# Sums of the second attention layer as two float32r products, and a reordered start, in a two-layer attention kernel

## The chip, the cores and the metric

One core of one Trainium2 chip runs the whole kernel. The metric is the device time of one execution in microseconds, from the first to the last instruction with what lies around them. All times below are in microseconds (us).

## The reference

Eight images of 32 x 32 positions (N = 1024 tokens) with 512 channels go through two layers. Each layer is x + attention(group norm(x)). The first has 16 heads of 32 channels, a bias-free qkv projection and an output projection w_proj. The second has 4 heads of 128 channels, projections Wq, Wk, Wv, Wo, and adds relative position logits (one term from the column offset, one from the row offset) to the scores ahead of the softmax:

```python
# layer 0
attn = softmax((q * SCALE) @ k.T);  x = x + (attn @ v) @ w_proj + b_proj
# layer 1
q = groupnorm(x) @ Wq * scale
scores = q @ k + relative_logits(q, pos_emb_w, pos_emb_h)
x = x + (softmax(scores) @ v) @ Wo
```

Everything is float32. The part that the change touches is the denominator of the second layer's softmax: for each query the sum of exp(score) over 1024 keys.

## The kernel before

**Layout.** Activations lie transposed in SBUF, channels on the 128 partitions, in four chunks (cc) of 1024 tokens. Every projection is a two-by-two block product done in seven instead of eight products (`seven`, with the combinations that `forms` makes on DVE, L332 to L335). Its matmuls are all issued in `by_columns` (L312), 32 columns of weights at a time. The weight combinations are made once at the start: `Matrix.fetch` loads a 512 x 512 weight (L135), `Matrix.add_up` subtracts quarters (four operations, L146) and stores the result to DRAM (L148) for later streaming (`Stream`, L198).

**Batches.** The eight images (batches) go through as a software pipeline. While attention_0 (first layer) of one batch runs, pieces of the neighbours' projections are dealt in between by costs (`side_by_side`). attention_1 (second layer) yields a cost of 0 in every step, so that it runs as one block, with attention_0 standing still. Woven into the block is only the loading of the next batch (`load`: DVE transposes L710, statistics L248/L249, group norm L274 to L292, forms), a piece every few steps. Blocks 1 to 6 in time have such a load beside them; the last two have not.

**attention_1.** Eight groups: head h (4) times half c of the queries (2), and in each eight steps j over the keys. A step is, on PE: two products into a PSUM bank, k times q (L647, fp32) and the position logits (L648, float32r); then, for the step before, v times e into the accumulator acc (L659, fp32). ACT takes exp of the bank into e (L650). DVE adds the e's of a group up in es (L668, L670). When a group's eight steps are through, ACT copies acc to q (L673), the product of an all-ones matrix and es (L679) sums es over the partitions, and `normalise` follows: ACT copies the sums (su, L495), DVE transposes, inverts, checks and transposes back (L497 to L513), POOL multiplies q by it (L517). The banks for ps, acc and sums come from a pool "bank" of three; the tag "ps", a tile of four banks, holds attention_0's logits. The snapshots su and tu have a tag "rec" with two buffers.

**Order.** The program is emitted in Python order, generators being stepped as described; then a scheduler sets each engine's own order, by what is ready. Each engine takes its list strictly in turn and waits at semaphores. In the resulting lists before the change, L679 stands on PE after the first L659 of the next group; at the end of a block (`run` of the last `finish`) it stands right after the last L659. After the block PE goes on with a projection (x_q, x_wp or x_wo) or, for the last batch, with x_wo, whose later products y_wo need the forms f_ao of the normalised q.

**Start.** `load_first` loads batch 0 by rows (x_rows), turns it on PE into PSUM banks (L737), copies the banks to x0T (ACT L745, DVE L747), takes statistics, puts x0T away to DRAM on SP's queue (`put_away`, L217, four stores d<-x0T) and runs group norm (L292 in place on x0T, four times) and forms. Then WV0's, WQ0's and WK0's combinations are made: WV0's on POOL, the others' on DVE, each stored by POOL's queue. The first products (x_v, y_v, z_v: the values of batch 0) follow; their a_v is L372.

**The end.** After the last block: x_wo products, then su, tu, rc, su (L495 to L513), POOL's L517 on q, the forms f_ao, and y_wo, z_wo. `Onto.gather` adds products to x2T on POOL (L431) and DVE (L436), and the rows go out (L835, L840).

Of the kernel before, what the change touches and what calls it, by code (L numbers as in the profile page):

```python
# [9 lines left out]
F32 = mybir.dt.float32  # L10
F32R = mybir.dt.float32r
# [6 lines left out]
P = 128  # L18
# [9 lines left out]
def quick_path(  # L28
# [23 lines left out]
    nc = tc.nc  # L52
# [3 lines left out]
    CC = C // P  # L56
    NT = N // P
    NB = 512
# [3 lines left out]
    HB = P // D0  # L62
# [4 lines left out]
    consts = ctx.enter_context(tc.tile_pool(name="consts", bufs=1))  # L67
    mem = ctx.enter_context(tc.tile_pool(name="mem", bufs=1))
    small = ctx.enter_context(tc.tile_pool(name="small", bufs=1))
    psum = ctx.enter_context(tc.tile_pool(name="psum", bufs=1, space=PSUM))  # L70
# [4 lines left out]
    def block(name, shape=None, dtype=F32):  # L75
        return mem.tile(shape or [P, CC, N], dtype, tag="block", name=name, bufs=BLOCKS)

    def chunks(block):
        return [block[:, i, :] for i in range(CC)]

    def bank(name, shape=None):
        return psum.tile(shape or [P, NB], F32, tag="bank", name=name, bufs=3)
# [1 line left out]

    ident = consts.tile([P, P], F32, tag="ident", name="ident")
    make_identity(nc, ident)
    ones = consts.tile([P, P], F32, tag="ones", name="ones")
    nc.gpsimd.memset(ones, 1.0)
    bproj_sb = consts.tile([P, CC], F32, tag="bproj_sb", name="bproj_sb")
    with nc.allow_non_contiguous_dma(reason="512 values, once"):  # L90
        nc.gpsimd.dma_start(bproj_sb, b_proj.rearrange("(cc p) -> p cc", p=P))
# [212 lines left out]
    in_place = [False]  # L304

    half_done = [None]

    def by_columns(out, weights, moving, start, stop, open_sum=False):

        for g in range(P // 32):  # L310
            columns = slice(32 * g, 32 * g + 32)
            ins = nc.tensor.matmul(  # L312
                out[columns, :],
                weights[:, columns],
                moving,
                start=start,
                stop=stop,
                skip_group_check=open_sum,
            )
            if in_place[0]:  # L320
                tc.keep_in_program_order(ins)
        in_place[0] = False

    def forms(x, name):


        a11, a12 = x[:, :HC, :NB], x[:, HC:, :NB]
        a21, a22 = x[:, :HC, NB:], x[:, HC:, NB:]
        s1, s2, s4 = [
            mem.tile([P, HC, NB], F32, tag=f"form{i}", name=f"f{i}_{name}", bufs=1) for i in (1, 2, 4)  # L330
        ]
        nc.vector.tensor_add(s1, a21, a22)  # L332
        nc.vector.tensor_sub(s2, s1, a11)  # L333
        nc.vector.tensor_sub(a21, a11, a21)
        nc.vector.tensor_sub(s4, a12, s2)  # L335
        return [a11, a12, s4, a22, s1, s2, a21]

    def snapshot(tag, name):
# [150 lines left out]
    def normalise(dst, acc_sums, name):  # L489

        su = mem.tile([P, NB], F32, tag="rec", name=f"su_{name}", bufs=2)
        nc.scalar.copy(su, acc_sums)  # L495
        turned = mem.tile([P, NB], F32, tag="rec", name=f"tu_{name}", bufs=2)
        nc.vector.transpose(turned, su)  # L497
        few = turned.rearrange("p (t c) -> p t c", c=32)[:, :, 0]
        rec = mem.tile([P, NB // 32], F32, tag="few", name=f"rc_{name}", bufs=2)
        nc.vector.reciprocal(rec, few)  # L500
        at = check_at[0]
        check_at[0] += 1
        nc.vector.tensor_tensor_reduce(
            out=few,
            in0=few,
            in1=rec,
            op0=ALU.add,
            op1=ALU.max,
            scale=1.0,
            scalar=0.0,  # L510
            accum_out=checks[:, at : at + 1],
        )
        nc.vector.transpose(  # L513
            su.rearrange("p (t c) -> p t c", c=32),
            rec.unsqueeze(2).to_broadcast([P, NB // 32, 32]),
        )
        nc.gpsimd.tensor_tensor(dst, dst, su, op=ALU.mult)  # L517
# [119 lines left out]
    def attention_1(q, k, v, posT, b):  # L637

        steps = [(h, c, j) for h in range(H1) for c in range(NH) for j in range(NT)]
        state = {}  # L640

        def front(h, c, j):
            name = f"1_{b}_{h}_{c}_{j}"
            ps = bank(f"ps_{name}")
            keys = slice(j * P, (j + 1) * P)
            queries = slice(c * NB, (c + 1) * NB)
            nc.tensor.matmul(ps, k[h][:, keys], q[:, h, queries], start=True, stop=False)  # L647
            nc.tensor.matmul(ps, sel_flat[:, keys], posT[:, h, queries], start=False, stop=True)  # L648
            e = mem.tile([P, NB], F32, tag="e1", name=f"e_{name}", bufs=3)
            nc.scalar.activation(e, ps, AF.Exp, scale=1.0 / math.sqrt(D1))  # L650
            return e

        def back(h, c, j, e):
            name = f"1_{b}_{h}_{c}_{j}"
            if j == 0:
                state["acc"] = bank(f"acc_{name}")
                state["first"] = e
            acc = state["acc"]
            nc.tensor.matmul(  # L659
                acc,  # L660
                v[:, j, h * D1 : (h + 1) * D1],
                e,
                start=(j == 0),
                stop=(j == NT - 1),
            )
            if j == 1:
                state["esum"] = mem.tile([P, NB], F32, tag="es1", name=f"es_{name}", bufs=2)
                nc.vector.tensor_add(state["esum"], state["first"], e)  # L668
            elif j > 1:
                nc.vector.tensor_add(state["esum"], state["esum"], e)  # L670
            if j < NT - 1:
                return
            nc.scalar.copy(q[:, h, c * NB : (c + 1) * NB], acc)  # L673
            state["ended"] = (h, c, state["esum"])

        def finish(h, c, esum):
            name = f"1_{b}_{h}_{c}"
            su = bank(f"sums_{name}")
            nc.tensor.matmul(su, ones, esum, start=True, stop=True)  # L679
            normalise(q[:, h, c * NB : (c + 1) * NB], su, name)  # L680

        pending = None
        for at in steps:
            e = front(*at)
            ended = state.pop("ended", None)
            if pending is not None:
                back(*pending)
            pending = (*at, e)
            if ended is not None:
                finish(*ended)  # L690
            yield 0
        back(*pending)
        yield 0
        finish(*state.pop("ended"))

    def load(b, st):

# [21 lines left out]
    def load_first(st):  # L719

        rows = block("x_rows", [P, NT, C])
        for t in range(NT):
            queue = nc.scalar if t % 2 else nc.sync
            queue.dma_start(rows[:, t, :], xf[0, t * P : (t + 1) * P, :])
        WV0.fetch(nc.sync)
        x = block("x0T_0")
        xT = chunks(x)
        for h in range(NH):
            if h == 0:
                whole = psum.tile([P, CC, NB], F32, tag="ps", name="turned_0", bufs=1)  # L730
                banks = [whole[:, cc, :] for cc in range(CC)]
            else:
                banks = [bank(f"turned_1_{cc}") for cc in range(CC - 1)]
                banks.append(psum.tile([P, NB], F32, tag="acc", name="turned_1", bufs=1))
            for t in range(NT // NH):
                for cc in range(CC):
                    nc.tensor.transpose(  # L737
                        banks[cc][:, t * P : (t + 1) * P],
                        rows[:, h * (NT // NH) + t, cc * P : (cc + 1) * P],
                        ident,  # L740
                    )
            for cc in range(CC):
                part = xT[cc][:, h * NB : (h + 1) * NB]
                if h == 0 or cc % 2:
                    nc.scalar.copy(part, banks[cc])  # L745
                else:
                    nc.vector.tensor_copy(part, banks[cc])  # L747

        idle = psum.tile([P, CC, NB], F32, tag="ps", name="idle", bufs=1)
        for t in range(6):  # L750
            nc.tensor.matmul(idle[:, t % CC, :], ident, rows[:, t, :], start=True, stop=True)
        for cc in (1, 0, 3, 2):
            statistics(st, xT, cc, "0_0")
        st["kept"] = put_away(xT, "0_0")
        run(group_norm(st, xT, "0_0"))
        st["xn"] = forms(x, "xn0_0")

    def before_first(st):
# [99 lines left out]
    def run(part):  # L858
        for _ in part:
            pass  # L860
# [53 lines left out]

    states = [{} for _ in range(B)]
    load_first(states[0])
    WV0.add_up(nc.gpsimd, nc.gpsimd, keep=True)
    for m in (WQ0, WK0):
        m.fetch(nc.sync)
        m.add_up(nc.vector, nc.gpsimd, keep=True)  # L920
    fill_sel()
    stream = Stream(plan)

# [12 lines left out]
    for b in range(B + 1):  # L936
        rest, total = [], 0
# [531 lines left out]
```

## Time and profile before

| what | value |
|---|---|
| runs | 3903.57, 3906.62, 3903.42 (median 3903.57) |
| profiled execution | 3902.0 |
| its span, first to last instruction | 3900.2 |
| busy: PE, DVE, ACT, POOL | 3806.4, 2517.3, 1725.1, 621.7 |
| granted TensorE clock, mean | 0.995 |
| L679 sums, records x mean | 128 x 0.592 |
| L648 float32r logits, records x mean | 512 x 0.794 |
| L650 exp on ACT, count x mean | 512 x 0.598 |
| L670 es on DVE, count x mean | 384 x 0.760 |
| L495 copy on ACT, count x mean | 128 x 0.586 |

An fp32 matmul leaves two records (two halves that follow each other), a float32r matmul one. Matmuls are pipelined, so the length of a record isn't what a matmul costs: that is read from the distance of two starts. In a timeline line the columns are start, duration, engine, source line, operation, output and inputs, partitions x elements, count, and in brackets the idle time before it and what ended it. In a line of waits the three numbers are the total, how many, and the longest. The lines of the kernel's profile carry the numbers of the code above (L679 is line 679).

### The profile page before, as it was taken

Reading aid. Unit: us, or ns where it says so; the run is one execution under the profiler, and the core shown is the slowest. Engines: PE = TensorE matmul, PEld = TensorE weight load, DVE = VectorE, ACT = ScalarE, POOL = GpSimd, SP = SyncE. Lnnn points to the kernel's source line nnn. Section 1 sums busy time; section 2 is a strip of 40 time slices with the busy share of each in tenths; the row PEclk is TensorE's granted clock in tenths of the full one; section 3 lists DMA queues with packets and bytes.
Section 4 is the critical chain, followed back from the end, with each engine's and each line's share of the span. In section 5 each row is a group of like instructions: output and inputs, shape, how many; then the busy total and the mean of one; then the engine's idle time right before and its main releaser. Section 6 shows DMA issues by size and latency. Waiting matters only on the chain. (4 is left out here: it accounts for less than half of the span.)

```text
span 3900.2 us, 79833 instructions
## 1 busy us (share of the span) xinstructions
PE 3806.4 (98%) x34478; PEld 1370.9 (35%) x34478; DVE 2517.3 (65%) x2905; ACT 1725.1 (44%) x1767; POOL 621.7 (16%) x400
## 2 busy tenths in 40 slices
PE   8999899999999999999999999999999999999998
PEld 3222244232442224432343323433234332244353
DVE  5777675576745867468664686656865568754544
ACT  2554553445434454344544445344453445643132
POOL 1341001121101211012111121111210112011101
PEclk9999999999999999999999999999999999999999
DMA  5221120133202322023120241103311123110401
GB/s 172 86 95 51 40 61 3 39 117 70 59 5 63 107 57 55 12 91 84 46 55 17 92 94 40 44 24 97 88 45 32 31 92 69 32 63 18 124 17 23
DMA packets 482984, 234.73 MB, mean 60 GB/s; under 512 B 269600, under 2 KB 461376, under 8 KB 481600
## 3 DMA queue, kind: packets, MB, share of 16 engines
q1 hardware_dynamic: 470992, 213.74, 20.3%
q0 software_dynamic: 2608, 13.70, 1.0%
q8 instruction: 274, 4.49, 0.5%
q10 hardware_dynamic: 9024, 2.10, 0.3%
q14 instruction: 86, 0.70, 0.1%
HBM read 170.72 MB, written 58.72 MB: 59 GB/s over the span
## 5 line engine op out<-in xcount | busy, mean ns | idle before, releaser
L540 ACT ACTIVATE e<-ps 128x2048 f32<-128x2048 f32 x512 | 961.7, 1878 | 844.6 <-PE ps L532 605.9
L562 DVE TENSOR_TENSOR es<-es,e 128x2048 f32<-128x2048 f32 x384 | 890.8, 2320 | 400.2 <-ACT e L540 397.4
L532 PE MATMUL ps<-q,k 32*64 32x512 f32 x8192 | 577.2, 615 | 36.4 <-ACT e L540 36.3
L650 ACT ACTIVATE e<-ps 128x512 f32<-128x512 f32 x512 | 305.9, 598 | 585.9 <-PE ps L648 549.1
L551 PE MATMUL acc<-e,v 128*32 128x512 f32 x4096 | 547.1, 606 | 0.4 <-ACT su L495 0.4
L647 PE MATMUL ps<-q,k 128*128 128x512 f32 x1024 | 523.6, 593 | 0.4 <-DVE posT L633 0.4
L659 PE MATMUL acc<-e,v 128*128 128x512 f32 x1024 | 521.9, 592 | 0.0
L517 POOL TENSOR_TENSOR q<-q,su 128x512 f32<-128x512 f32 x128 | 214.3, 1674 | 1564.8 <-DVE su L513 1538.1
L670 DVE TENSOR_TENSOR es<-es,e 128x512 f32<-128x512 f32 x384 | 291.8, 760 | 264.0 <-ACT e L650 262.5
L648 PE MATMUL ps<-posT,sel 128*128 128x512 f32 x512 | 406.6, 794 | 0.0
L647 PEld LDWEIGHTS ps<-q,k 128*128 128x128 f32 x1024 | 193.6, 190 | 246.2 <-issue 240.6
L532 PEld LDWEIGHTS ps<-q,k 32*64 32x64 f32 x8192 | 120.4, 130 | 432.4 <-ACT e L540 217.0
L659 PEld LDWEIGHTS acc<-e,v 128*128 128x128 f32 x1024 | 193.1, 189 | 146.7 <-issue 105.0
L551 PEld LDWEIGHTS acc<-e,v 128*32 128x32 f32 x4096 | 81.5, 108 | 413.4 <-issue 365.8
L560 DVE TENSOR_TENSOR es<-e,e 128x2048 f32<-128x2048 f32 x64 | 174.7, 2730 | 39.7 <-ACT e L540 39.7
L497 DVE STREAM_TRANSPOSE tu<-su 128x512 f32<-128x512 f32 x128 | 90.6, 708 | 136.2 <-ACT su L495 136.0
L495 ACT COPY su<-sums 128x512 f32<-128x512 f32 x128 | 75.1, 586 | 151.3 <-PE sums L572 83.4
L648 PEld LDWEIGHTS ps<-posT,sel 128*128 128x128 f32 x512 | 97.3, 190 | 122.5 <-issue 122.5
L668 DVE TENSOR_TENSOR es<-e,e 128x512 f32<-128x512 f32 x64 | 44.2, 691 | 145.7 <-ACT e L650 145.7
L633 DVE TENSOR_TENSOR posT<-pp,posT 32x512 fp32r<-32x512 f32 x128 | 112.0, 875 | 32.2 <-ACT posT L628 30.8
L421 POOL TENSOR_TENSOR k<-b_k,p_k 128x512 f32<-128x512 f32 x32 | 51.2, 1599 | 477.0 <-ACT p_k L386 474.9
L628 ACT CAST posT<-pp 32x512 fp32r<-32x512 f32 x128 | 106.0, 828 | 45.2 <-PE pp L615 44.1
(195 smaller groups left out, 4510.1 us busy)
## 6 DMA issues: line engine op xcount, KB each, us to landing
w_qkv<-ws_qkv SPq DMA_DIRECT2D x168, 128.0 KB, 2.5
d<-x0T SPq DMA_DIRECT2D x32, 512.0 KB, 3.6
x1T<-d SPq DMA_DIRECT2D x32, 512.0 KB, 5.5
d<-x1T SPq DMA_DIRECT2D x32, 512.0 KB, 3.6
x2T<-d SPq DMA_DIRECT2D x32, 512.0 KB, 5.9
w_qkv<-in_L_conv_w_qkv SPq DMA_DIRECT2D x126, 128.0 KB, 2.2
out<-ot SPq DMA_DIRECT2D x240, 64.0 KB, 2.0
xs<-in_x SPq DMA_DIRECT2D x224, 64.0 KB, 2.6
```

Of the source, the lines that this page charges most:

```text
L517: nc.gpsimd.tensor_tensor(dst, dst, su, op=ALU.mult)
L532: nc.tensor.matmul(ps[some, r, :], k[m][rows, j * P + 64 * i : j * P + 64 * i + 64], q[m][rows, h * NB : (h + 1) * NB], start=True, stop=True,
L540: nc.scalar.activation(e, ps, AF.Exp, scale=D0 ** -0.5)
L551: nc.tensor.matmul(acc[r * D0 : (r + 1) * D0, :], v[:, j, c0 : c0 + D0], e[:, r, :], start=(j == 0), stop=(j == NT - 1),)
L560: nc.vector.tensor_add(state["esum"], state["first"], e)
L562: nc.vector.tensor_add(state["esum"], state["esum"], e)
L633: nc.vector.tensor_sub(rest, logits, greater)
L647: nc.tensor.matmul(ps, k[h][:, keys], q[:, h, queries], start=True, stop=False)
L648: nc.tensor.matmul(ps, sel_flat[:, keys], posT[:, h, queries], start=False, stop=True)
L650: nc.scalar.activation(e, ps, AF.Exp, scale=1.0 / math.sqrt(D1))
L659: nc.tensor.matmul(acc, v[:, j, h * D1 : (h + 1) * D1], e, start=(j == 0), stop=(j == NT - 1),)
L670: nc.vector.tensor_add(state["esum"], state["esum"], e)
```

## The change

In `attention_1` the sum of es over the partitions is no longer one fp32 product. `finish` becomes a generator: one step after the group's end, ACT copies es into a float32r tile (sg, the rounded part) and DVE subtracts it (sr, the rest); two steps later, PE takes the sum as two float32r products, all-ones times sg and all-ones times sr, accumulated in one bank. That bank is the first of the tile with tag "ps". At the end of a block all of `finish` is run at once. In PE's list the pair stands after the fourth L659 of the next group; at the end of a block, after one matmul of the projection that follows. In ACT's list sg stands ahead of the next group's first exp, and su behind its fourth; in DVE's list sr stands behind the last es of its group, and tu to su some two to three steps later than before. sg and sr take buffers of the tag "rec". The all-ones tile gets the type float32r and is read as fp32 elsewhere.

At the start, all eight copies of the turned batch 0 to x0T are made on ACT (before: six on ACT, two on DVE), the statistics go over the chunks in the order 0, 2, 1, 3, and the weight combinations of WQ0 and WK0 on DVE are issued behind the last operation of the first forms (`issue_after`). In the lists this moves the eight L146 of DVE behind the forms, where four of them stood among statistics and group norm and two among the forms; it moves the load of WK0 on SP's queue ahead of the four stores d<-x0T, and POOL's second store of combinations behind rstd (L289). At the ends of the last two batches POOL's L431 on p_wo or p_wp stands ahead of the last L517 instead of behind it.

```diff
@@ -84,8 +84,9 @@
 
     ident = consts.tile([P, P], F32, tag="ident", name="ident")
     make_identity(nc, ident)
-    ones = consts.tile([P, P], F32, tag="ones", name="ones")
-    nc.gpsimd.memset(ones, 1.0)
+    ones_r = consts.tile([P, P], F32R, tag="ones", name="ones")
+    nc.gpsimd.memset(ones_r.bitcast(F32), 1.0)
+    ones = ones_r.bitcast(F32)
     bproj_sb = consts.tile([P, CC], F32, tag="bproj_sb", name="bproj_sb")
     with nc.allow_non_contiguous_dma(reason="512 values, once"):
         nc.gpsimd.dma_start(bproj_sb, b_proj.rearrange("(cc p) -> p cc", p=P))
@@ -304,6 +305,7 @@
     in_place = [False]
 
     half_done = [None]
+    last_form = [None]
 
     def by_columns(out, weights, moving, start, stop, open_sum=False):
 
@@ -332,7 +334,7 @@
         nc.vector.tensor_add(s1, a21, a22)
         nc.vector.tensor_sub(s2, s1, a11)
         nc.vector.tensor_sub(a21, a11, a21)
-        nc.vector.tensor_sub(s4, a12, s2)
+        last_form[0] = nc.vector.tensor_sub(s4, a12, s2)
         return [a11, a12, s4, a22, s1, s2, a21]
 
     def snapshot(tag, name):
@@ -675,23 +677,38 @@
 
         def finish(h, c, esum):
             name = f"1_{b}_{h}_{c}"
-            su = bank(f"sums_{name}")
-            nc.tensor.matmul(su, ones, esum, start=True, stop=True)
+
+            yield
+
+            greater = mem.tile([P, NB], F32R, tag="rec", name=f"sg_{name}", bufs=2)
+            nc.scalar.copy(greater, esum)
+            rest = mem.tile([P, NB], F32R, tag="rec", name=f"sr_{name}", bufs=2)
+            nc.vector.tensor_sub(rest, esum, greater.bitcast(F32))
+
+            yield
+            yield
+
+            su = psum.tile([P, HB, NB], F32, tag="ps", name=f"sums_{name}", bufs=1)[:, 0, :]
+            nc.tensor.matmul(su, ones_r, greater, start=True, stop=False)
+            nc.tensor.matmul(su, ones_r, rest, start=False, stop=True)
             normalise(q[:, h, c * NB : (c + 1) * NB], su, name)
 
         pending = None
+        ending = []
         for at in steps:
             e = front(*at)
-            ended = state.pop("ended", None)
             if pending is not None:
                 back(*pending)
             pending = (*at, e)
-            if ended is not None:
-                finish(*ended)
+            for part in ending:
+                next(part, None)
+            if "ended" in state:
+                ending = [finish(*state.pop("ended"))]
+                next(ending[0])
             yield 0
         back(*pending)
         yield 0
-        finish(*state.pop("ended"))
+        run(finish(*state.pop("ended")))
 
     def load(b, st):
 
@@ -739,17 +756,14 @@
                         rows[:, h * (NT // NH) + t, cc * P : (cc + 1) * P],
                         ident,
                     )
-            for cc in range(CC):
+            for cc in (0, 2, 1, 3):
                 part = xT[cc][:, h * NB : (h + 1) * NB]
-                if h == 0 or cc % 2:
-                    nc.scalar.copy(part, banks[cc])
-                else:
-                    nc.vector.tensor_copy(part, banks[cc])
+                nc.scalar.copy(part, banks[cc])
 
         idle = psum.tile([P, CC, NB], F32, tag="ps", name="idle", bufs=1)
         for t in range(6):
             nc.tensor.matmul(idle[:, t % CC, :], ident, rows[:, t, :], start=True, stop=True)
-        for cc in (1, 0, 3, 2):
+        for cc in (0, 2, 1, 3):
             statistics(st, xT, cc, "0_0")
         st["kept"] = put_away(xT, "0_0")
         run(group_norm(st, xT, "0_0"))
@@ -917,7 +931,9 @@
     WV0.add_up(nc.gpsimd, nc.gpsimd, keep=True)
     for m in (WQ0, WK0):
         m.fetch(nc.sync)
-        m.add_up(nc.vector, nc.gpsimd, keep=True)
+
+        with tc.issue_after(last_form[0].ins):
+            m.add_up(nc.vector, nc.gpsimd, keep=True)
     fill_sel()
     stream = Stream(plan)
 
```

## The prediction

> **What bounds the kernel now.** I read the busy shares first, then the chain of waits and PE's own list of waits, then the instruction groups and the timelines of the places that the change touches.
>
> ```profile
> PE 3806.4 (98%) x34478; PEld 1370.9 (35%) x34478; DVE 2517.3 (65%) x2905; ACT 1725.1 (44%) x1767; POOL 621.7 (16%) x400
> ```
>
> PE is busy for 98% of the span and the chain of waits runs along PE, so a saved PE slot is saved time, as long as nothing else comes late there. PE's waits are few:
>
> ```profile
> PE ps L532 <- ACT e L540: 36.3, 30, 7.6
> PE y_wo L312 <- DVE a_wo L372: 11.2, 9, 1.7
> PE x_v L312 <- issue: 9.3, 1, 9.3
> ...
> PE y_wo L312 <- DVE f_ao L333: 3.1, 1, 3.1
> ```
>
> The longest row belongs to attention_0, which the change leaves alone. The 9.3 us is the start, and the last row the end (3861 to 3865 us); both are touched. In attention_1 PE waits for nothing that counts. Its steps, from the PE timeline of the seventh group of batch 7:
>
> ```profile
> 3809.18 1.02 PE L659 MATMUL acc<-e,v 128*128 128x512 f32 x2
> 3810.04 1.02 PE L679 MATMUL sums<-es,ones 128*128 128x512 f32 x2
> 3810.90 1.02 PE L647 MATMUL ps<-q,k 128*128 128x512 f32 x2
> 3811.35 0.80 PE L648 MATMUL ps<-posT,sel 128*128 128x512 f32 x1
> 3811.99 0.59 PE L659 MATMUL acc<-e,v 128*128 128x512 f32 x1
> ```
>
> Ends overlap, so I price by starts. L679 starts 0.86 after L659, and L647 0.86 after L679: an fp32 product of 512 columns takes a slot of 0.857. From L647 (3810.90) to L659 (3811.99) is 1.09; less L647's own 0.857 leaves 0.233 for L648, the float32r product, though its record says 0.80. A group of eight steps repeats every 16.433 us = 8 x 1.947 + 0.857 (a step is 2 x 0.857 + 0.233).
>
> **What the skill says.** "FP8 and Floating Point Precision", TensorE Precision Notes: true FP32 takes four passes through the array, and reduced-precision FP32 reads a truncated value. The trace agrees: 0.857 / 0.233 = 3.7. "SBUF — State Buffer", Terms: VectorE and GpSimd share a port pair, held for a whole instruction, and "the loser fully blocks". The trace agrees: the L333 that starts at 595.34, while POOL's L517 runs from 595.00 for 1.56, takes 2.30 where its like takes 1.21. "PSUM — Partial Sum Buffer", Engine vs sequencer instructions: the queues of ScalarE, VectorE and GpSimd are strict FIFO. In the trace, too, the records of each keep the order of the instruction list; that rule decides steps 2 to 4 below.
>
> **Step 1, the 56 sums inside a block (8 batches, 7 each).** One fp32 product goes; two float32r products come, after the fourth L659 of the next group, two steps later. The idle bank they use is attention_0's logits tile, which is free in this block. 0.857 - 2 x 0.233 = 0.391, times 56 = **-21.9 us**. The trace has no two float32r products back to back. If the second overlaps less (0.32, midway to a full fp32 half), it is -17; if each is its 0.21 (a fourth of 0.857), -24.
>
> ScalarE gets a copy (sg, 0.59 as its other 512-column copies) and DVE a subtraction (sr, 0.60 to 0.69 as L670). Neither is a bound in the block: an exp of 0.60 each 1.947 us on ACT. What counts is the place in the queues (steps 2 to 4).
>
> **Step 2, the seven block ends before the last.** There the sums follow one product of the next projection, and the last es (L670) now has two operations behind it. Before:
>
> ```profile
> 682.65 0.69 DVE L670 TENSOR_TENSOR es<-es,e 128x512 f32<-128x512 f32 x1 [1.25 <-ACT e L650]
> 682.67 0.30 PEld L659 LDWEIGHTS acc<-e,v 128*128 128x128 f32 x2 [0.66 <-ACT e L650]
> 683.40 0.43 PEld L679 LDWEIGHTS sums<-es,ones 128*128 128x128 f32 x2 [0.43 <-DVE es L670]
> 683.64 1.02 PE L679 MATMUL sums<-es,ones 128*128 128x512 f32 x2
> ```
>
> The sums end their slot at 683.64 + 0.857 = 684.50. After: es ends 683.34; sg 683.42 to 684.01; sr 684.06 to 684.75; weights and handing over 0.29; the second float32r slot 0.23: 685.27. The cost is 0.77 each, and PE has only one matmul to put into it: 7 x 0.77 = **+5.4 us** (4 to 6).
>
> **Step 3, the last block's end.** Here su, tu, rc, su and POOL's L517 lead to the forms (L332, L333) for which y_wo waits. The sums come 0.77 later; the instruction order also puts POOL's L431 (x2T += p_wo) ahead of the last L517. L431 waits for the ACT copy p_wo (L367), which ended at 3859.93 and moves to about 3860.5; L431 1.27, then L517 1.28: 3863.1 instead of 3861.48. **+1.65 us** (0.8 to 3.3: PE's clock fell to half right after the 3.15 us gap there, and a longer gap may cost another such stretch). In batch 6 the same order of POOL is hidden behind other work of PE.
>
> **Step 4, sg stands in front of an exp.** In ACT's list sg stands ahead of the next group's first exp, and waits for es of step 7 on DVE. Queued behind it are that exp and the copy q (L673); PE's L659 waits for the exp. Elsewhere es of step 7 ends 0.72 after the last exp, in 58 of the 64 groups (the DVE and ACT timelines). sg then ends 0.72 + 0.08 + 0.59 = 1.39 after it; the next exp starts, in the trace, 1.35 after. A delay of 0.06 against 1.15 us that its L659 leaves: nothing. In the six blocks beside which the next batch is loaded (553 to 3052 us), the third group is different. DVE has the forms there:
>
> ```profile
> 597.56 0.68 DVE L670 TENSOR_TENSOR es<-es,e 128x512 f32<-128x512 f32 x1
> 598.16 1.21 DVE L334 TENSOR_TENSOR x0T<-x0T 128x1024 f32<-128x1024 f32 x1
> 599.30 0.68 DVE L670 TENSOR_TENSOR es<-es,e 128x512 f32<-128x512 f32 x1
> 599.90 1.21 DVE L335 TENSOR_TENSOR f_xn<-x0T,f_xn 128x1024 f32<-128x1024 f32 x1
> 601.04 1.48 DVE L670 TENSOR_TENSOR es<-es,e 128x512 f32<-128x512 f32 x2
> ```
>
> es ends 602.51, 2.05 after exp 7 (600.46); it hurt nobody, as the sums came two steps later. sg may start only then. With the lag L, sg ends L + 0.67 after exp 7, and PE is late by L + 0.67 + 0.02 - 1.35 - 1.08 (its 1.15 less 0.07 of handing over) = L - 1.74. What is L after the change? DVE gains sr of the group before (0.60), and the chain tu to su (1.8) with POOL's product behind it moves two steps later, so that the product meets L334 instead of L333 and costs its 1.1 where DVE has no idle time left (at L333 it had some 0.7 before). I take 2.05 + 0.60 + 0.35 = 3.0, a stall of 1.3, with a handing over of 0.1: 1.4 x 6 = **+8.4 us**. Ends: L unchanged 0.3 x 6 = 2; 0.60 + 1.1 more, 2.1 x 6 = 13.
>
> **Step 5, the start.** DVE loses two copies L747 (0.68 each) to ACT, which then has 8 instead of 6 in a row (some 0.55 each), and takes all eight L146 of WQ0 and WK0 out from among the statistics, group norm and forms. One of them waited there:
>
> ```profile
> 16.61 0.69 DVE L146 TENSOR_TENSOR prep_qkv<-prep_qkv 128x512 f32<-128x512 f32 x1 [1.97 <-DMA prep_qkv<-in_L_conv_w_qkv]
> ...
> 24.63 2.98 DVE L292 TENSOR_SCALAR x0T<-x0T,back,rstd 128x1024 f32<-128x1024 f32 x4 [1.17 <-POOL rstd L289]
> ```
>
> Without it rstd could be ready at about 20, 4 us sooner. But L292 writes x0T in place, so each of its four waits until its d<-x0T store has read. On SP's queue WK0's load of 1 MB, which stood behind the four stores, now stands ahead of them; the DMA engines are full from 8 to 28 us, and the 1 MB took 2.8 us of data. The stores landed at 17.85, 19.08, 20.48, 21.86; I put them at 20.6, 21.9, 23.4 and 24.6 to 27. The last L292 then ends at 25 to 27.5 (before 27.61), the forms lose two L146 between them (1.2), but eight L146 (5.2 us) now lie ahead of a_v (L372), behind PE work that fills most of that. Net **-1.0 us** (-3 to +1). POOL's store of WQ0's sums moves behind rstd, and with it SP's loads of sums (w_qkv<-ws_qkv) and the next xs behind those; they have until about 66 us, which covers up to 15 us of delay.
>
> **Sum.** -21.9 + 5.4 + 1.65 + 8.4 - 1.0 = -7.5 us. The profiled execution took 3902.0 (span 3900.2, 1.8 around it), the runs' median is 3903.57; the same difference from it gives 3896.1.
>
> **Rivals.**
> (a) The DVE work of the six third groups finds its own gaps, so L stays near 2.1 and step 4 costs 2: 3889.7. For it: DVE is idle for a third of the span. Against it: those four forms run without a gap in the lines above.
> (b) Slower: sg's wait reaches the ordinary transitions too. The place is ACT in front of exp 0; the price is L - 1.74 at each of the 50 others; it decides from L = 1.74 on, against 0.72 now, that is when sr, the shifted transposes and POOL's product put 1 us more before es. At a stall of 0.4 each, +20 us: 3916. Against it: an ordinary step uses 0.60 to 0.69 of 1.947 us of DVE, and the added chain of 1.8 us ends some two steps before es of step 7.
> (c) The change doesn't do what it says: the two float32r products take the 0.857 of the fp32 one (each 0.43, if the pair doesn't stream like L648 behind an fp32 product). Step 1 is then nothing: +14.4, 3918. Against it: the slot of L648 is 0.233 in every step.
> (d) The start turns round: stores held behind WK0 and the eight L146 ahead of a_v cost 3 instead of giving 1: 3900.
>
> **How the numbers follow.** About 0.2% (7.8 us) is what a measurement of this kernel can tell from no change, so faster means below 3895.8. The forecast lies at that border: its case (chance 0.60) is 3890.5 to 3902, half on each side. Rival (a) 0.20 (3886 to 3892), (d) 0.10 (3897 to 3904), (b) 0.06, (c) 0.04. Faster: 0.20 + 0.28 = 0.48; same: 0.32 + 0.10 = 0.42; slower: 0.10. The range 3887 to 3903 leaves out the ends of (a), of (d), and (b) and (c).
>
> **What would show it.** Step 1: starts from L659 over the pair to L647, 0.47 instead of 0.86. Step 2: x_q begins 0.7 to 0.8 us later after the last L659 of a block. Step 4: a PE row "acc L659 <- ACT e L650" of about 8 us, six times; if it is absent, (a); if it has 50 entries, (b). Step 3: y_wo's wait for f_ao L333 some 4.8 instead of 3.1. Step 5: first x_v, forms and a_v against 25.55, 28.13 and 34.48. I am wrong if the pair costs over 0.6, or if the stall of step 4 shows elsewhere than in the third groups.

## The result and the profile after

The changed kernel takes 3897.6 us (median of four runs, 3890.95 to 3900.83) against 3903.49: ratio 0.9981, 95% interval 0.9964 to 0.9999. A second set of 21 runs of it gave 3895.46 against 3903.87: ratio 0.9983, interval 0.9976 to 0.9989. That is 6 to 8 us less, near the forecast of 3896.1 and at the border of 0.2% that the prediction named.

The profiled execution shows only 1.5 us of it (span 3898.7 against 3900.2). Both numbers can be right, because PE's granted clock differs between executions. The lines below are from the table by windows (columns: window, length, busy time and count of PE, PEld, DVE, ACT and POOL, granted clock, DMA share, GB/s), first before, then after:

```profile
3420.00:3440.00 20.00, 17.58 (x260) 6.34 (x256) 15.58 (x14) 9.38 (x7) 4.38 (x2) 1.00 0.10 26
3640.00:3660.00 20.00, 17.02 (x164) 5.32 (x160) 8.75 (x13) 2.35 (x4) 1.28 (x1) 1.00 0.59 125
```

```profile
3420.00:3440.00 20.00, 17.59 (x244) 6.16 (x240) 13.90 (x9) 9.27 (x6) 4.38 (x2) 0.91 0.10 28
3640.00:3660.00 20.00, 17.08 (x148) 5.34 (x144) 6.35 (x10) 2.23 (x4) 1.28 (x1) 0.91 0.63 139
```

A clock of 0.91 over 20 us is one stretch of 3.4 us at half speed, 1.7 us of time lost. Yet both kernels have the same gap in PE's work ahead of the first of these stretches, first before, then after:

```profile
3426.77 1.12 PE L532 MATMUL ps<-q,k 32*64 32x512 f32 x16 [2.42 <-ACT e L540]
```

```profile
3424.65 1.96 PE L534 MATMUL ps<-q,k 32*64 32x512 f32 x16 [2.41 <-ACT e L542]
```

After the gap the 16 products take 1.12 us before and 1.96 us after.

The trace records when the clock was halved. Over the whole span such stretches cost 20.5 us before and 25.3 after, but part of them lies where PE has nothing to do. Counted only where PE has work between 60 us and its last matmul, they cost 7.9 us before and 14.6 after, 6.7 more. The Trainium skill, "TensorE: Matmul & The Clock Gate" (What's actually happening), says that the clock is halved after an idle window of about 3.4 us and restored after a busy one, and that this window of 3413 ns is free-running: it "doesn't reset when your kernel starts". The traces agree on the window. In the twelve profiles of this case, every stretch between 60 us and the last matmul is 3.41, 6.83 or 10.24 us long, one, two or three windows, and the windows start at another moment in each. They differ on the idle: no window has to be wholly idle. Each of the 74 stretches follows a gap between PE's records of at least 2.1 us. I laid the windows out from the edges of the stretches. Of those at full clock, all 63 in which PE had no record for more than 2.02 us of the 3.41 were followed by half clock, none with less than 1.43 us was, and of those between 11 of 83 were.

So the stretches don't lie just anywhere. Before and after, PE has the same ten gaps of over 2 us behind 60 us, and only the last changes in length by over 0.1 us (3.15 to 3.65 us, ahead of y_wo). Which of the gaps are followed by half clock depends on where the windows happen to fall, and that differs between executions of one and the same kernel. So I read the steps from the shifts of PE's instructions within stretches of full clock, and the totals from the medians.

PE's waits after the change:

```profile
PE ps L534 <- ACT e L542: 35.2, 28, 7.6
PE y_wo L314 <- DVE a_wo L374: 11.6, 9, 1.8
PE acc L661 <- ACT e L652: 7.2, 6, 1.2
PE x_v L314 <- issue: 6.0, 1, 6.0
...
PE y_wo L314 <- DVE f_ao L335: 3.7, 1, 3.7
```

The third row is new: six waits of 1.2 us for an exp, once in each block with a load beside it. The start waits 6.0 instead of 9.3 us; y_wo at the end 3.7 instead of 3.1. The pair itself, from PE's timeline in the same group as the lines of before:

```profile
3810.48 1.02 PE L661 MATMUL acc<-e,v 128*128 128x512 f32 x2
3810.93 0.80 PE L692 MATMUL sums<-sg,ones 128*128 128x512 f32 x1
3811.57 0.40 PE L693 MATMUL sums<-sr,ones 128*128 128x512 f32 x1
3811.81 1.02 PE L649 MATMUL ps<-q,k 128*128 128x512 f32 x2
```

From L661 to L649 is 1.33; less L661's own 0.857, the pair takes 0.47, as against 0.857 for the fp32 product. And the new wait, from the timeline (all engines) of the first block:

```profile
598.73 1.56 POOL L519 TENSOR_TENSOR q<-q,su 128x512 f32<-128x512 f32 x1 [10.51 <-DVE su L515]
...
599.08 2.29 DVE L337 TENSOR_TENSOR f_xn<-x0T,f_xn 128x1024 f32<-128x1024 f32 x1
...
601.29 1.47 DVE L672 TENSOR_TENSOR es<-es,e 128x512 f32<-128x512 f32 x2
602.86 0.62 ACT L684 CAST sg<-es 128x512 fp32r<-128x512 f32 x1 [3.23 <-DVE es L672]
603.38 0.59 ACT L652 ACTIVATE e<-ps 128x512 f32<-128x512 f32 x1
...
604.02 1.12 PE L661 MATMUL acc<-e,v 128*128 128x512 f32 x2 [1.14 <-ACT e L652]
```

Read it from the top: the last es comes late on DVE (behind a form that, beside POOL's product, takes 2.29 instead of 1.22), ACT stands idle for 3.23 us until sg may start, the exp behind sg is late, and PE waits 1.14 us for it. The collision of POOL and DVE isn't new: in the same block before, it fell on L333 (2.30, shown in the prediction).

### The profile page after: what moved, and what is told of

It reads as the page before. It is cut to its first block, busy times and chain, and to the rows that moved or that the text cites. A ratio compares the mean times of both kernels' runs of the same rounds, so it can differ in the third digit from the quotient of the medians.

```text
span 3898.7 us, 79896 instructions
## 1 busy us (share of the span) xinstructions
PE 3800.2 (97%) x34478; PEld 1377.3 (35%) x34478; DVE 2555.3 (66%) x2967; ACT 1761.0 (45%) x1833; POOL 618.3 (16%) x400
## 4 chain that ended last, share of the span: by engine, by line
## 5 line engine op out<-in xcount | busy, mean ns | idle before, releaser
L661 PE MATMUL acc<-e,v 128*128 128x512 f32 x1024 | 522.6, 593 | 7.2 <-ACT e L652 7.2
L649 PE MATMUL ps<-q,k 128*128 128x512 f32 x1024 | 523.7, 593 | 0.3 <-DVE posT L635 0.3
L672 DVE TENSOR_TENSOR es<-es,e 128x512 f32<-128x512 f32 x384 | 283.1, 737 | 275.9 <-ACT e L652 275.1
L519 POOL TENSOR_TENSOR q<-q,su 128x512 f32<-128x512 f32 x128 | 209.6, 1638 | 1563.6 <-DVE su L515 1562.8
L649 PEld LDWEIGHTS ps<-q,k 128*128 128x128 f32 x1024 | 193.8, 190 | 224.1 <-issue 212.0
L661 PEld LDWEIGHTS acc<-e,v 128*128 128x128 f32 x1024 | 192.9, 189 | 155.7 <-issue 91.5
L423 POOL TENSOR_TENSOR v<-b_v,p_v 128x512 f32<-128x512 f32 x32 | 50.8, 1587 | 440.6 <-ACT p_v L388 437.9
```

The lines of the kernel that those rows point to most:

```text
L661: nc.tensor.matmul(acc, v[:, j, h * D1 : (h + 1) * D1], e, start=(j == 0), stop=(j == NT - 1),)
```

## The experiments

**The two halves of the change apart.** `start_only` is the kernel before with the edits of the start; `sums_only` is the changed kernel with the start of before.

```diff
 # start_only, against before
-            for cc in range(CC):
+            for cc in (0, 2, 1, 3):
...
+                nc.scalar.copy(part, banks[cc])
...
+        with tc.issue_after(last_form[0].ins):
+            m.add_up(nc.vector, nc.gpsimd, keep=True)
 # sums_only, against after: these lines the other way round
```

> The kernel before with the edits of the start alone. Theory A (the sum of steps, each in its own place): the first x_v comes some 3.4 us sooner, but L292 still waits for the stores of x0T, and eight L146 stand ahead of a_v, so that the values, and all that follows, come 0.6 us sooner: 3902.9 against 3903.5. Theory B (the start carries the gain): 3.4 us and more: 3900 or less.

> The sums of the second layer as in the changed kernel, the start as before. Theory A: -21.9 for the 56 pairs, +8.6 to 9 for the six third groups, +6.3 for the eight block ends, about +1 behind the last one: some -6 to -7, 3896.5 to 3897.5. Theory B (the start carries the gain): near 3901 or more, since the sums give nothing.

Measured: start_only 3901.03, ratio 0.9994 (0.9985 to 1.0002); sums_only 3896.97, ratio 0.9988 (0.9980 to 0.9996), both against 3903.17. The start alone can't be told from no change by its time. In its trace PE's instructions between 60 and 100 us, ahead of the first differing clock stretch, stand 1.3 us earlier than before, with the whole change 0.6 (the spread of such numbers is under step 5 below). The interval of sums_only lies below 1: the sums carry most of the gain. The two intervals overlap, so that the times alone don't rank the halves; the shifts in the traces do. The same six waits stand in sums_only (7.2 us), so they belong to the sums.

**sg out of the exp's way.**

```diff
-            nc.scalar.activation(e, ps, AF.Exp, scale=1.0 / math.sqrt(D1))
+            state["exp"] = nc.scalar.activation(e, ps, AF.Exp, scale=1.0 / math.sqrt(D1))
...
-            nc.scalar.copy(greater, esum)
+            with tc.issue_after(state["exp"].ins):
+                nc.scalar.copy(greater, esum)
```

> The changed kernel, with sg put behind the second exp of the next group on ACT instead of ahead of the first. Theory A: the wait of PE for exp in the six third groups (7.2 us of waits, some 8.7 of shift) goes and nothing takes its place, as the pair stands two steps later: 8 to 9 us less than the changed kernel, some 3888 to 3889. Rival: the wait moves on, sr comes too late for the pair or the later su and POOL's product block something else: then within 2 us of the changed kernel.

Measured: 3888.69, ratio 0.9961 (0.9947 to 0.9974), wholly below the interval of the changed kernel's 21 runs. Its list of PE's waits has no row for acc behind exp; the place in the first block (DVE, ACT and PE's weight loads):

```profile
600.85 2.29 DVE L337 TENSOR_TENSOR f_xn<-x0T,f_xn 128x1024 f32<-128x1024 f32 x1
602.72 0.60 ACT L652 ACTIVATE e<-ps 128x512 f32<-128x512 f32 x1 [1.35 <-PE ps L650]
603.07 1.48 DVE L672 TENSOR_TENSOR es<-es,e 128x512 f32<-128x512 f32 x2
...
605.16 0.61 ACT L685 CAST sg<-es 128x512 fp32r<-128x512 f32 x1
```

DVE is as late as it was (the last es ends at 604.55, the form takes 2.29 again), but the exp no longer waits for it, and the pair two steps later doesn't either. The lateness of DVE costs nothing here; the place in ACT's queue made it cost. Each loaded block now gains 2.72 us, as the unloaded ones do.

**The same copy made by DVE.**

```diff
-            nc.scalar.copy(greater, esum)
+            nc.vector.tensor_copy(greater, esum)
```

> The changed kernel with the rounded copy sg made by DVE instead of ACT, so that nothing on ACT stands in front of the next exp. Theory A (the stall is ACT's queue, not DVE's load): the six waits of PE for exp go, and 8 to 9 us with them; at the block ends the copy is as long as on ACT, so nothing changes there: some 3888 to 3889. Rival (DVE is the late one, whoever makes the copy): the extra 0.6 of DVE in each group makes es, sr or the pair late, and the third groups still stall: 3895 to 3898.

Measured: 3888.20, ratio 0.9964 (0.9951 to 0.9978); all of its five runs lie below all 21 of the changed kernel taken beside them (3887.36 to 3889.13, against 3891.59 to 3901.79). The six waits are gone here too, though DVE has one operation more in each group and the last es of the third group is up to 0.35 us later than in the changed kernel. That settles between the queue and DVE's load: the queue. At the block ends it is as slow as the change (the shift there is again 0.78).

**Block ends as before.**

```diff
-        run(finish(*state.pop("ended")))
+        h, c, esum = state.pop("ended")
+        su = bank(f"sums_1_{b}_{h}_{c}")
+        nc.tensor.matmul(su, ones, esum, start=True, stop=True)
+        normalise(q[:, h, c * NB : (c + 1) * NB], su, f"1_{b}_{h}_{c}")
```

> The changed kernel, with the last group of each block summed by one fp32 product straight from es, as before; the other 56 sums stay pairs. Theory A: 8 x 0.78 = 6.2 us come back, and POOL's last product stands ahead of L431 again (about 1 us more at the end): some 6.5 to 7 less than the changed kernel, near 3890.5. Rival: the fp32 product costs at the ends what the pair's wait did, because PE waits for es anyhow: within 2 us of the changed kernel.

Measured: 3889.81, ratio 0.9962 (0.9948 to 0.9975). The six waits for exp are still there (7.2 us), and y_wo's wait for the forms is back from 3.7 to 3.1 us. So the two losses have places of their own. At an end nothing covers sg and sr: the fp32 product from es is the shorter way.

**Both.** The two edits above together.

> The changed kernel with sg behind the second exp and, at the block ends, one fp32 product. Theory A: only the 56 pairs (-21.9) and the start (-0.6) are left: 22.5 less than before, some 3881. Rival: the two losses share their cause (DVE late), so taking both away gives little more than one of them: 3886 to 3889.

Measured: 3879.54 against 3900.68, ratio 0.9942 (0.9929 to 0.9956): some 21 to 22 us, the sum of what is left. In its trace all eight blocks gain 2.71 us or more, and every end is as long as before. The losses add.

**WK0's load behind the stores.** SP's queue nearly as it was before the change (one small load, 64 KB of xs, now also stands ahead of the stores), everything else of the changed kernel kept:

```diff
-            nc.sync.dma_start(d, xT[cc])
+            last_store[0] = nc.sync.dma_start(d, xT[cc])
...
-        m.fetch(nc.sync)
+        with tc.issue_after(last_store[0].ins) if m is WK0 else nullcontext():
+            m.fetch(nc.sync)
```

> The changed kernel with the load of WK0 behind the four stores of x0T on SP's queue, as it was before the change. Theory A (the stores hold L292 back): L292's four operations run through at about 20.7 to 23.7 instead of 21.3 to 28.2, forms and the eight L146 come 4 us sooner, and 3 to 4 us are left at the first attention: some 3894. Rival: the load of x0T's norm is not what counts, the eight L146 ahead of a_v or PE's half clock are: within 1 us of the changed kernel's start.

Measured: 3891.87, ratio 0.9976 (0.9967 to 0.9986). That interval overlaps the changed kernel's (0.9976 to 0.9989), so the gain has to be read from the traces. In DVE's timeline the changed kernel waits four times for the stores before it may write x0T in place; the variant waits once, for rstd. First the changed kernel, then the variant:

```profile
21.27 0.81 DVE L293 TENSOR_SCALAR x0T<-x0T,back,rstd 128x1024 f32<-128x1024 f32 x1 [1.75 <-DMA d<-x0T]
22.42 0.81 DVE L293 TENSOR_SCALAR x0T<-x0T,back,rstd 128x1024 f32<-128x1024 f32 x1 [0.34 <-DMA d<-x0T]
24.56 0.81 DVE L293 TENSOR_SCALAR x0T<-x0T,back,rstd 128x1024 f32<-128x1024 f32 x1 [1.33 <-DMA d<-x0T]
27.43 0.81 DVE L293 TENSOR_SCALAR x0T<-x0T,back,rstd 128x1024 f32<-128x1024 f32 x1 [2.06 <-DMA d<-x0T]
```

```profile
20.31 2.98 DVE L295 TENSOR_SCALAR x0T<-x0T,back,rstd 128x1024 f32<-128x1024 f32 x4 [1.17 <-POOL rstd L292]
```

a_v starts at 32.81 instead of 37.76, and PE between 60 and 100 us stands 4.05 us earlier than before, instead of 0.6. That is more than profiles of one start differ by: the first x_q begins at 49.05 here and at 48.15 in the next kernel, against 51.79 to 52.68 in the eight profiles with the changed start. So most of the gain that the start's other edits prepared was taken by the load of WK0, which is first read by one of the eight L146, at 32.95 us or later.

**All three.**

> All three: sg behind the second exp, fp32 sums at the block ends, and WK0's load behind the stores. Theory A: 3 to 4 us below the kernel with the first two, some 3877 to 3878. Rival: as above, no gain from the load: 3881.

Measured: 3877.41 against 3900.68, ratio 0.9934 (0.9921 to 0.9948). PE stands 4.9 us earlier between 60 and 100 us than before, against 0.4 in the kernel with two edits. That kernel has the latest start of the eight profiles; against their mean the gain is 4.0. The medians of the two kernels differ by only 2.1 us and their intervals overlap, so the medians alone don't show the load's part here. This kernel is faster than the kernel before and than the changed one: its interval lies wholly below that of the changed one (0.9976 to 0.9989).

**One product only.** The rest sr and its product are left out; the 56 sums are those of the rounded es.

```diff
-            rest = mem.tile([P, NB], F32R, tag="rec", name=f"sr_{name}", bufs=2)
-            nc.vector.tensor_sub(rest, esum, greater.bitcast(F32))
...
-            nc.tensor.matmul(su, ones_r, greater, start=True, stop=False)
-            nc.tensor.matmul(su, ones_r, rest, start=False, stop=True)
+            nc.tensor.matmul(su, ones_r, greater, start=True, stop=True)
```

> As with sg behind the second exp and fp32 sums at the block ends, but the rest sr and its product are left out, so that the 56 sums are those of the rounded es alone. Prices the second product. Theory A: 56 x 0.233 = 13.0 us less than the same with both products: some 3868. Rival: the pair is cheaper together than two slots (the second has the same weights): 56 x 0.21 = 12 or less; or dearer than two, 56 x 0.32 = 18.

Measured: 3862.74 against 3900.68, ratio 0.9903 (0.9887 to 0.9918), 16.8 below the kernel with both edits. In the traces a block of seven sums is 1.73 us shorter, 0.247 for each second product, 13.8 for 56; the medians of four and five runs don't fix the difference to better than some us, and where the other 3 us lie is not shown. The pair is two slots, 0.22 and 0.247: neither the common weights nor the second place make it clearly cheaper than two single products of 0.233.

**The change once more,** beside the DVE variant.

> The changed kernel itself, in the same session as the last variant. Theory A: the sum of steps is -7.1 for the profiles once the half-clock stretches are taken out, so the median should stand 6 to 8 us below that of before. Rival: the stretches of half clock belong to the change (its gaps bring them on), so the difference stays as small as in the first profiles, 1 to 3 us.

Measured: 3895.46, ratio 0.9983 (0.9976 to 0.9989). Its profile has 22.4 us lost to the clock over the span, between before (20.5) and the first profile of the change (25.3), with the same six waits and the same gaps. Over all runs the mean granted clock is 0.9944 in the 25 of the kernel before and 0.9945 in the 21 of the changed one. The difference comes to less than 1 us of a run, so the rival is out: the change doesn't bring more half clock on in sum. The one gap that it lengthens, ahead of y_wo, is followed by two windows of half clock in four of the six profiles that have it at 3.65 us, and by none in the other two; at 3.1 us it is followed by one window in all six.

## Why the prediction was right, step by step

- **Step 1, the pair (-21.9).** Right. In the last two blocks, which have no load beside them, PE gains 2.72 us over seven sums: 0.389 each (I had 0.391), 21.8 for 56. Rival (c), a pair as dear as the fp32 product, is out.
- **Step 2, block ends (+5.4).** Right. The sixteenth record of the next projection starts 3.49 us after the block's last record of acc, before 2.71: 0.78 each, 5.5 for seven. The first end after the change (the lines of before are in the prediction):

```profile
682.06 0.62 ACT L684 CAST sg<-es 128x512 fp32r<-128x512 f32 x1 [0.81 <-DVE es L672]
682.36 1.04 PE L314 MATMUL x_q<-x0T,w_qkv 128*32 128x512 f32 x2
...
682.78 0.69 DVE L686 TENSOR_TENSOR sr<-es,sg 128x512 fp32r<-128x512 f32 x1 [0.81 <-ACT sg L684]
...
683.34 0.51 PE L692 MATMUL sums<-sg,ones 128*128 128x512 f32 x1
...
683.68 0.39 PE L693 MATMUL sums<-sr,ones 128*128 128x512 f32 x1
...
684.00 1.06 PE L314 MATMUL x_q<-x0T,w_qkv 128*32 128x512 f32 x8
```

  PE has one product of x_q to put into the time that sg and sr take.
- **Step 3, the last end (+1.65).** Right in its mechanism, 1.28 at y_wo (from the block's last record of acc to y_wo 10.41 instead of 9.13 us). POOL's L433 did go first, 3857.08 to 3858.36, and L519 behind it. What I had not seen: before, that POOL addition ran beside L332 and stretched it to 2.27; now the form takes 1.23. DVE then put a ready addition (0.68) between the forms, which took part of that back. One more window of half clock follows there in this profile, within what I allowed.
- **Step 4, sg ahead of exp (+8.4).** Right in place, count and price, lucky in L. There are 1.2 us of wait six times, and in shifts 1.23 to 1.33 gained per loaded block instead of 2.72, 8.8 in all. The price L - 1.74 holds: the lag L of es is 3.14 in the first block (exp 7 ends at 599.63, es at 602.76) and 3.22 in the other five, and the shifts lost are 1.40 and 1.48. But L didn't grow as I wrote, by 0.60 for sr and 0.35 for the collision. Before and after, DVE works without a break from L292 (after: L293) of the group norm to the last es, in the first block for 14.39 and 14.51 us, and no sr lies in that time. Counted from the block's start, es ends only 0.30 us later there (0.39 in the other blocks); exp 7 ends 0.78 earlier, because two pairs have by then saved PE 0.39 each. I had left out that the change itself moves exp 7 forward while DVE stays. The two errors nearly cancel. The form that POOL's product hits is the fourth (L337 after) in the first block only; in the other five it is the third (L336), as I wrote. Rival (a), DVE finding its own gaps, and rival (b), a stall at the ordinary transitions, would have left no row or fifty; the row has six.
- **Step 5, the start (-1.0).** Right in sign and mechanism: -0.6 in this pair of profiles, where the stores hold L293 until 28.24 (before 27.61), and the first x_v's lead of 3.4 us is gone by 60 us. Eight profiles have the changed start and two the old one; by the first x_q their means differ by 1.0 us. In the eight, x_q begins 24.25 to 24.30 us after the last L293 ends, wherever the clock was halved there, so DVE's chain behind L293 (forms, eight L146, a_v) sets it and not the clock. With the old start it was 25.49, and L292 ended 0.2 us earlier on average. Rival (d) took the same mechanism a step too far.

The sum by measured terms is -21.8 + 5.5 + 1.3 + 8.8 - 0.6 = -6.8. The clock adds 6.7 us to the first profile, -0.1, where its span shows -1.5; most of the rest lies between the first x_q and the first block of attention_1, where the time without a PE record ranges from 27.0 to 29.4 us over the twelve profiles (before 29.4, after 28.5). For the second profile of the change the start gave -0.9, so the terms are -7.1, and the clock adds 1.8: -5.3, where its span shows -5.8. The medians give -5.9 and -8.4.

The prediction gave the clock a term at the end of the kernel only. It is rather the noise around every term: the 25 runs of the kernel before in the second set reach from 3897.6 to 3908.0 us, and their spans are 3898.6 us on average at a granted clock of 0.995 and 3903.0 at 0.994.

## What to carry to other kernels

A float32r pair for an fp32 product with an exact all-ones operand pays 0.39 us for 512 columns in this kernel, where PE is the bound, but only where its two preparing operations are covered: at the end of a block, with nothing beside it, the pair loses 0.78 us, twice what it gains elsewhere. Ask of each added copy what stands behind it in its engine's queue: a late input that hurt nobody becomes a stall if its reader is put ahead of something urgent. A faster engine meets the slower one sooner: here part of the stall came from PE's own gain. And a load put ahead of stores on one queue delayed the operation that waited to overwrite the stored buffer.

## What the runs showed of the hardware

A float32r copy of 128x512 on ACT is recorded as a cast and takes 0.619, an fp32 one from PSUM 0.586. Of the two float32r products in a row the first has a record of 0.80 and the second of 0.40, while their slots are 0.22 and 0.25 (0.47 less 0.247): here the record of a matmul behind an fp32 one says little of what it costs. When a DVE form of 128x1024 starts while POOL's product of 128x512 runs, both are longer in these traces, the form 2.29 instead of 1.22 and the product 1.56 instead of 1.28; the prediction priced the one that starts second only. The half-clock stretches of a run of some 3900 us sum to 18.8 to 27.0 us lost over the twelve profiles, of which 9.7 to 20.1 fall where PE has work; each of their windows costs up to 1.7 us. They follow gaps in PE's work of 2.1 us and more, and the 109 gaps of 1.3 to 2 us behind 60 us were followed by none.
